# A transformer block in fp32: two token tiles per step in one projection, an earlier start in the other, and a residual handed to ScalarE and Pool

## The chip, the cores and the metric

The kernel runs on one core of a Trainium2 chip. A core has five engines that this document names: TensorE (PE; its weight loads are listed apart as PEld), VectorE (DVE), ScalarE (ACT), Pool (POOL) and the queue of DMA issues SP. Each engine works through its own instructions in order and waits on semaphores for the others. The metric is the time of one execution on the device in microseconds (us), as the median of several.

## The reference

The input is `h` of shape 8 x 1024 x 512, in fp32: eight sequences of 1024 tokens with 512 features. Every sequence goes through a block with a norm before and after each part:

```python
x = h
x = x + layernorm(attention(layernorm(x), Wqvk, Wo))
x = x + layernorm(ffn(layernorm(x), W1, b1, phases, w_real, w_imag, W2, b2))

# attention: 16 heads of 32 features, causal, softmax(q k / sqrt(512)) v, then Wo
# ffn:
hidden = x @ W1 + b1                                   # 512 -> 2048
imag   = w_imag * sin(phases + 0.1 * hidden)
phase  = cos(phases) * w_real + sin(phases) * w_imag   # per feature
act    = relu(hidden + 0.1 * phase * imag)
y      = act @ W2 + b2                                 # 2048 -> 512
```

`layernorm` subtracts the mean over the 512 features and divides by the root of the variance plus 1e-5; it has no weights of its own.

## The kernel before

The sequences are worked on one after the other. A token tile is 128 tokens (128 partitions) by 512 features, so a sequence has 8 tiles and a half of a sequence has 4. The running `x` of a sequence lies in SBUF in 8 tiles.

**Attention** (`attention`, L666) takes the 16 heads in 4 groups of 4 heads (`g` = 0 to 3). A group has two stages. `find_maxima` (L434) multiplies queries and keys once to get the row maxima: TensorE writes scores into PSUM banks (L473), VectorE reduces them with the mask (L503) or without (L491), ScalarE takes exponentials for one half (L523), and `split` brings the maxima into three bf16 parts, for one half on Pool (L451 to L460), which TensorE then transposes (L106). Four runs of this stage are filled up with steps of `work`, the projection of queries, keys and values for the next group (L374, L395). The second stage multiplies again with the maxima already subtracted, in units of key blocks: 3 units for the first half of the queries (`c` = 0), 7 for the second (`c` = 1), counted through as `at` = 0 to 9. For each unit `weigh` does the product (L577, L588), the exponential on ScalarE (L603) and on Pool the causal cut of the diagonal blocks (a select, L607). `weighted_values` (L626) follows one unit later. In the second half VectorE adds the weights of all units up (`add_weights`, L655); at the end of the group TensorE sums them over keys with a matmul of ones (L641), and `divide` takes Ln and Exp on ScalarE and multiplies on VectorE (L660 to L663). In a group that is not the last this happens inside the first run of the next group's maxima.

**The projection with Wo and the norms around it** (`finish_block`, L751) exist once for each half. For each of the 4 tiles: TensorE projects (L761), ScalarE copies the result out of PSUM (L770), VectorE takes mean and variance (`moments`, L218 and L219), Pool computes the reciprocal root (`rstd_of`, L225 and L226, a pair of instructions), VectorE normalises (L230) and adds to `x` (L281); then mean and variance of the new `x`, again the pair on Pool, the normalisation into `xn` (L230), four transposes on TensorE (L106), and ScalarE's copy into `x2T` (L248), the right side of the feed-forward.

**The feed-forward** (`feed_forward`, L785) takes 16 chunks of 128 hidden features for each half, 32 in all. `hidden` multiplies with W1 (L806) and lets ScalarE and VectorE form the activation (L814 to L825); `accumulate` multiplies with W2 into four PSUM banks (L833), two chunks later (`LAG`). `end(half)` adds the bias b2 on VectorE (L847), normalises and adds to `x` (L230, L281), stores `x` to DRAM through SP and loads the next sequence's tile there (L853, L113).

**What sets the order.** Side work is written as generators: `staged` runs the stages of successive tiles one step apart, later stages first within a step, and `advance` takes one step of such work at a chosen place. Instructions marked `in_order` keep their place in the program on their engine; the others may be moved by the scheduler of the framework, which orders each engine's queue before the run. TensorE's instructions are all in order. Three pieces of side work matter here:

- `finish_block` for half 0 runs during group 3, one step after each unit from `at` = 4 on. It has 8 steps for 4 tiles, so six run in the units, one after them, and one after the sums.
- `finish_block` for half 1 (`between`) runs in the feed-forward, one step per chunk, after the accumulation:

```python
if c >= LAG:
    accumulate(c - LAG)
...
elif c > 1:
    advance(between)
    advance(rest)
```

- `end(1)` of a sequence is left over (`rest`) for group 0 of the next sequence. Its four bias additions are issued at the end of the feed-forward, its steps from `at` = 3 on (`if g == 0: return rest, len(KEY_UNITS[0])`).

The buffers for `yp`, `xn`, `yb`, `inverse` and reloaded input come from a pool of 5 tiles, those of weights, scores and hidden chunks from a pool of 7.

## Time and profile before

| | |
|---|---|
| Time, median of 3 runs | 3938.61 us (3938.57 to 3939.71) |
| The profiled execution | 3939.17 us, span of its instructions 3937.4 us |
| Granted TensorE clock | 0.997 of full speed |
| Busy: PE, DVE, ACT, POOL | 97%, 71%, 38%, 14% of the span |
| Start of the feed-forward, sequences 1 to 5 | 1269.25, 1755.55, 2241.86, 2728.16, 3214.46 us: one sequence takes 486.3 us |
| Chain that ended last, by engine | PE 85%, DVE 9%, ACT 2%, issue 2%, POOL 2% |
| Largest groups on PE | L806 919.0 us, L833 691.3 us, L374 480.9 us |

Lines of the profile read as follows. In the list of waits: the engine, what it wrote and on which line, an arrow to the one that released it, the sum of the idle time, how often, and the longest, in us. In the timeline: the start in us from the first instruction, the duration from the first to the last of a run of equal instructions, the engine, the line, the operation, what it writes and reads, the shapes, the count, and in brackets the idle time of the engine just before with what ended it. In the list of groups: the busy time of all, the mean duration of one in ns, and the idle time before them. An fp32 matmul stands as two instructions, so the four products of a tile show as x8. A matmul's end is modelled, so its duration overlaps the next one's start; the distance from start to start tells the pace.

### The profile page before, as it was taken

Reading aid. Unit: us, or ns where it says so; the run is one execution under the profiler, and the core shown is the slowest. Engines: PE = TensorE matmul, PEld = TensorE weight load, DVE = VectorE, ACT = ScalarE, POOL = GpSimd, SP = SyncE. Lnnn points to the kernel's source line nnn. Section 1 sums busy time; section 2 is a strip of 40 time slices with the busy share of each in tenths; the row PEclk is TensorE's granted clock in tenths of the full one; section 3 lists DMA queues with packets and bytes.
Section 4 is the critical chain, followed back from the end, with each engine's and each line's share of the span. In section 5 each row is a group of like instructions: output and inputs, shape, how many; then the busy total and the mean of one; then the engine's idle time right before and its main releaser. Section 6 shows DMA issues by size and latency. Waiting matters only on the chain.

```text
span 3937.4 us, 51398 instructions
## 1 busy us (share of the span) xinstructions
PE 3810.8 (97%) x19457; PEld 1759.9 (45%) x19457; DVE 2792.0 (71%) x6161; ACT 1504.8 (38%) x2804; POOL 545.7 (14%) x1131
## 2 busy tenths in 40 slices
PE   8999999999999999999999999999999999999998
PEld 4444444444444444444444444444444444444343
DVE  4777767777777777777777677766777766777666
ACT  4552145521465214642146421454214642155321
POOL 1220011200112001120012100111001120021200
PEclk9999999999999999999999999999999999999999
DMA  4000000000000001000000000000001000000000
GB/s 153 25 20 22 22 17 25 15 22 22 28 17 12 22 22 33 12 12 22 22 33 12 12 22 22 33 12 12 22 22 33 12 12 0 22 23 12 1 0 22
DMA packets 43496, 86.43 MB, mean 22 GB/s; under 512 B 4144, under 2 KB 4208, under 8 KB 42736
## 3 DMA queue, kind: packets, MB, share of 16 engines
q1 hardware_dynamic: 39056, 71.61, 5.6%
q10 hardware_dynamic: 4192, 11.53, 0.8%
q8 instruction: 152, 2.49, 0.3%
q14 instruction: 96, 0.79, 0.1%
HBM read 66.36 MB, written 16.78 MB: 21 GB/s over the span
## 4 chain that ended last, share of the span: by engine, by line
PE 85%; DVE 9%; ACT 2%; issue 2%; POOL 2%; DMA 0%; POOLq 0%; SPq 0%; DVEq 0%
PE banks L833 22%; PE banks L806 22%; PE banks L374 11%; PE banks L473 7%; PE banks L395 6%; PE banks L761 4%; PE banks L588 4%; PE banks L626 4%; DVE w L655 3%; PE banks L577 2%; DVE mx L491 2%; PE banks L106 2%; ACT w L603 1%; PE banks L641 1%; DVE st L218 1%
## 5 line engine op out<-in xcount | busy, mean ns | idle before, releaser
L806 PE MATMUL banks<-x2T,w_sb 128*128 128x512 f32 x2048 | 919.0, 593 | 5.4 <-ACT x2T L248 5.4
L833 PE MATMUL banks<-w_sb,hid 128*128 128x512 f32 x1536 | 691.3, 593 | 8.9 <-DVE hid L825 8.9
L603 ACT ACTIVATE w<-banks 128x1024 f32<-128x1024 f32 (+1 forms) x640 | 566.1, 937 | 284.4 <-PE banks L588 274.7
L806 PEld LDWEIGHTS banks<-x2T,w_sb 128*128 128x128 f32 x2048 | 386.0, 190 | 478.0 <-issue 468.8
L655 DVE TENSOR_TENSOR w<-w 128x1024 f32<-128x1024 f32 (+2 forms) x448 | 444.2, 1030 | 199.3 <-PE banks L626 168.3
L503 DVE CUSTOM_DVE_ANT_0 es<-banks,mask 128x128 f32<-128x128 f32 (+3 forms) x1024 | 432.6, 485 | 121.6 <-PE banks L473 121.6
L821 ACT ACTIVATE u<-u 128x512 f32<-128x512 f32 x256 | 161.1, 629 | 853.6 <-DVE u L189 853.5
L374 PE MATMUL banks<-xnT,wqvk_sb 128*128 128x512 f32 x1024 | 480.9, 609 | 3.0 <-DVE mx L491 3.0
L833 PEld LDWEIGHTS banks<-w_sb,hid 128*128 128x128 f32 x1536 | 291.2, 190 | 379.1 <-issue 335.1
L491 DVE TENSOR_REDUCE mx<-banks 128x1 f32<-128x512 f32 (+1 forms) x384 | 309.7, 861 | 116.9 <-PE banks L473 116.9
L607 POOL TENSOR_SCALAR_AFFINE_SELECT w<-w 128x256 f32<-128x256 f32 x512 | 292.6, 593 | 671.8 <-ACT w L603 664.1
L814 ACT ACTIVATE hid<-banks,prm 128x512 f32<-128x512 f32 x256 | 175.6, 686 | 502.2 <-PE banks L806 502.2
L626 PE MATMUL banks<-w,v 128*32 128x512 f32 (+3 forms) x3072 | 329.0, 496 | 22.8 <-POOL w L607 22.1
L588 PE MATMUL banks<-qk 32*128 32x512 f32 (+3 forms) x3072 | 327.9, 491 | 0.0
L816 DVE TENSOR_SCALAR u<-hid,prm 128x512 f32<-128x512 f32 x256 | 123.7, 483 | 282.5 <-ACT hid L814 282.1
L473 PE MATMUL banks<-qk 32*128 32x512 f32 (+3 forms) x3072 | 314.0, 513 | 0.3 <-DVE mx L503 0.2
L824 DVE SCALAR_TENSOR_TENSOR hid<-u,coef,hid 128x512 f32<-128x512 f32 x256 | 192.0, 750 | 162.7 <-ACT u L821 162.7
L374 PEld LDWEIGHTS banks<-xnT,wqvk_sb 128*128 128x128 f32 x1024 | 182.8, 190 | 243.3 <-issue 182.9
L523 ACT ACTIVATE es<-es,mx 128x512 f32<-128x512 f32 (+3 forms) x512 | 279.6, 550 | 2.0 <-DVE mx L503 2.0
L395 PEld LDWEIGHTS banks<-wqvk_sb,xnT 128*128 128x128 f32 x2048 | 239.0, 192 | 57.9 <-issue 34.4
L395 PE MATMUL banks<-wqvk_sb,xnT 128*128 128x128 f32 x2048 | 259.5, 280 | 0.0
L761 PE MATMUL banks<-wo_sb,wvT 128*128 128x512 f32 x512 | 233.5, 599 | 0.0
(96 smaller groups left out, 3371.2 us busy)
## 6 DMA issues: line engine op xcount, KB each, us to landing
xin<-in_L_attn_h_dram SPq DMA_DIRECT2D x112, 256.0 KB, 2.7
x<-in_L_attn_h_dram SPq DMA_DIRECT2D x64, 256.0 KB, 2.6
out_dram<-x SPq DMA_DIRECT2D x64, 256.0 KB, 2.0
w_tail<-in_L_ffn_W_dram SPq DMA_DIRECT2D x8, 1024.0 KB, 5.3
w_sb<-in_L_ffn_W_dram ACTq DMA_DIRECT2D x1, 4096.0 KB, 15.5
wqvk_sb<-in_L_attn_Wqvk_dram ACTq DMA_DIRECT2D x3, 1024.0 KB, 9.5
w_sb<-in_L_ffn_W_dram ACTq DMA_DIRECT2D x1, 3072.0 KB, 25.6
wo_sb<-in_L_attn_Wo_dram ACTq DMA_DIRECT2D x1, 1024.0 KB, 5.9
```

The lines of the kernel that those rows point to most:

```text
L374: nc.tensor.matmul(pq, wqvk_sb[:, kc, c0 : c0 + P], xnT[b, half][:, kc, :], start=(kc == 0), stop=(kc == KC - 1),)
L395: nc.tensor.matmul(pv[:, t - t0, :], xnT[b, t // TPB][:, kc, (t % TPB) * P : (t % TPB + 1) * P], wqvk_sb[:, kc, c0 : c0 + P], start=(kc == 0),
L473: nc.tensor.matmul(scs[j // 2][:, j % 2, at : at + n], t[r, 0, i * P : (i + 1) * P], t[r, 1, k0 : k0 + n], start=True, stop=True,)
L491: nc.vector.tensor_reduce(out=mx[:, m], in_=sc[:, m, cols], op=ALU.min, axis=mybir.AxisListType.X,)
L503: nc.vector.tensor_tensor_reduce(out=es[:, m, cols], in0=sc[:, m, cols], in1=mask[:, HALF - n :], scale=1.0, scalar=FMAX, op0=ALU.add, op1 ...
L588: nc.tensor.matmul(sts[j // 2][:, j % 2, cols], t[r, 1, kb * P : (kb + 1) * P], t[r, 0, q0 : q0 + n], start=False, stop=True,)
L603: in_order(nc.scalar.activation(w[:, :, :width], st[:, :, :width], AF.Exp, scale=-1.0))
L626: nc.tensor.matmul(acc[r, HALF - n :], v[b, g][:, kb, r], weights[j // 2][:, j % 2, cols], start=first and k == 0, stop=last and k == len( ...
L655: in_order(nc.vector.tensor_add(t[:, :, q], t[:, :, q], w[:, :, cols]))
L761: nc.tensor.matmul(y, wvT[:, kc, t * P : (t + 1) * P], wo_sb[:, kc, :], start=(kc == 0), stop=(kc == KC - 1),)
L806: nc.tensor.matmul(ph, w1_sb[:, kc, fc * P : (fc + 1) * P], x2T[half][:, kc, :], start=(kc == 0), stop=(kc == KC - 1),)
L833: nc.tensor.matmul(ys[half, t], hids[c // 2][:, c % 2, t * P : (t + 1) * P], w2_sb[:, fc, :] if fc < NW2 else w2_tail[:, fc - NW2, :], sta ...
```

## The change

Four things are done.

1. `finish_block` gets a parameter `by`, the number of tiles per step. Half 0 is done with two tiles per step: two projections in a row, one pair of Pool instructions for both tiles' roots, and so on. The measuring of the new `x` is a stage of its own. With 2 steps' worth of tiles and 5 stages there are 6 steps. Half 1 keeps one tile per step.
2. In the feed-forward the steps of half 1 begin with chunk 0 instead of chunk 2, and for the chunks 0 to 2 they stand before the accumulation instead of behind it.
3. `end(1)` of all sequences but the last (`spare`) copies the result out of PSUM on ScalarE, adds the bias on Pool and adds the normalised result to `x` on Pool. The copies and Pool's additions are in order.
4. In group 0 the steps of that residual are taken from the first run of the maxima on (four steps there, the other two from `at` = 3 on).

The normalisation stays on VectorE in all of them, and the sums, products and stores are the same as before. The diff, cut to its core:

```diff
@@ rstd_of
-            rs = small.tile([P, n], F32, tag=f"rs{n}", name="rs")
+            rs = small.tile([P, n], F32, tag=f"rs{n}", name="rs", bufs=4 // n)
@@ find_maxima, at the end of each of its four runs
             advance(work, fill)
+            advance(more)
@@ attention
         for g in range(NG):
-            mT, later = find_maxima(b, g, work, sums)
+            more, first = after(g)
+            mT, later = find_maxima(b, g, work, sums, more if g == 0 else iter(()))
             mTs = [mT]
-            more, first = after(g)
@@ finish_block
-        def project(t):
-            y = psum([P, D])
-...
-        measure, add = residual_stages(x, lambda t: ys[t])
-        return staged(
-            TPB,
-            lambda t: (project(t), measure(t)),
-            add,
-            *norm_stages(x, False, lambda t: x2T[half][:, :, t * P : (t + 1) * P], nc.scalar.copy),
-        )
+        def tiles(n):
+            return range(n * by, (n + 1) * by)
+
+        def measure(n, source):
+            mvs[n] = small.tile([P, by, 2], F32, tag=f"mv{by}", name="mv", bufs=6 // by)
+            for t in tiles(n):
+                moments(source(t), mvs[n][:, t - n * by, :])
+            rss[n] = rstd_of(mvs[n], by)
+
+        def project(n):
+            for t in tiles(n):
+                y = psum([P, D])
+                for kc in range(KC):
+                    in_order(nc.tensor.matmul(y, ...))
+                ys[t] = tmp.tile([P, D], F32, tag="tmp", name="yp")
+                nc.scalar.copy(ys[t], y)
+                drained(y)
+            measure(n, lambda t: ys[t])
+
+        def add(n):
+            for t in tiles(n):
+                in_order(normalise(n, t, ys[t], ys[t]))
+                in_order(nc.vector.tensor_add(x(t), x(t), ys[t]))
+
+        def scale(n):
+            for t in tiles(n):
+                xns[t] = tmp.tile([P, D], F32, tag="tmp", name="xn")
+                normalise(n, t, xns[t], x(t))
+
+        def transpose(n):
+            for t in tiles(n):
+                transpose_rows(xns[t], x2T[half][:, :, t * P : (t + 1) * P], nc.scalar.copy)
+
+        return staged(TPB // by, project, add, lambda n: measure(n, x), scale, transpose)
@@ feed_forward, end(half)
+            spare = half and b + 1 < B
...
-                nc.vector.tensor_add(yb, ys[half, t], b2_sb)
+                if spare:
+                    in_order(nc.scalar.copy(yb, ys[half, t]))
+                    in_order(nc.gpsimd.tensor_tensor(yb, yb, b2_sb, ALU.add))
+                else:
+                    nc.vector.tensor_add(yb, ys[half, t], b2_sb)
...
+            def add(t):
+                in_order(normalised(ybs[t], ybs[t], mvs[t], rss[t]))
+                if spare:
+                    in_order(nc.gpsimd.tensor_tensor(x(t), x(t), ybs[t], ALU.add))
+                else:
+                    in_order(nc.vector.tensor_add(x(t), x(t), ybs[t]))
@@ feed_forward, the loop over chunks c
             if c < 2 * NFC:
                 hidden(c)
+            if c <= LAG:
+                advance(between)
             if c >= LAG:
                 accumulate(c - LAG)
             if c - LAG == NFC - 1:
                 rest = end(0)
-            elif c > 1:
+            elif c > LAG:
                 advance(between)
                 advance(rest)
@@ the two calls
-                return finish_block(b, 0, wvT[0], x2T), len(KEY_UNITS[0]) + 1
+                return finish_block(b, 0, wvT[0], x2T, 2), len(KEY_UNITS[0]) + 1
...
-        rest = feed_forward(b, x2T, finish_block(b, 1, wvT[1], x2T))
+        rest = feed_forward(b, x2T, finish_block(b, 1, wvT[1], x2T, 1))
```

More of the change, by code (lines that the diff above doesn't have):

```diff
@@ L249, in transpose_rows, with norm_stages @@
         drained(pt)
-    def norm_stages(source, own, dst, evacuate):
+    def norm_stages(source, dst, evacuate):
         mvs, rss, xns = {}, {}, {}
@@ L261, in scale @@
         def scale(t):
-            xns[t] = source(t) if own else tmp.tile([P, D], F32, tag="tmp", name="xn")
+            xns[t] = tmp.tile([P, D], F32, tag="tmp", name="xn")
             normalised(xns[t], source(t), mvs[t], rss[t])
@@ L268, in norm_stages @@
         return measure, scale, transpose
-    def residual_stages(target, y):
-        mvs, rss = {}, {}
-        def measure(t):
-            mvs[t] = one_mv()
-            moments(y(t), mvs[t][:, 0, :])
-            rss[t] = rstd_of(mvs[t], 1)
-        def add(t):
-            in_order(normalised(y(t), y(t), mvs[t], rss[t]))
-            in_order(nc.vector.tensor_add(target(t), target(t), y(t)))
-        return measure, add
     def advance(work, steps=1):
@@ L317, in norm1_first @@
         dst = new_xnT(0)
-        return staged(NT, *norm_stages(lambda t: xt[0, t], False, dst, nc.scalar.copy))
+        return staged(NT, *norm_stages(lambda t: xt[0, t], dst, nc.scalar.copy))
     moments_ahead = {}
@@ L432, with find_maxima @@
     )
-    def find_maxima(b, g, work, sums):
+    def find_maxima(b, g, work, sums, more):
         t = qk[b, g]
@@ L749, in attention, with finish_block @@
             finish(more)
-    def finish_block(b, half, wvT, x2T):
+    def finish_block(b, half, wvT, x2T, by):
         x2T[half] = tp.tile([P, KC, HALF], F32, tag="t", name=f"x2T_{b}_{half}")
-        ys = {}
-        def project(t):
-            y = psum([P, D])
-            for kc in range(KC):
-                in_order(
-                    nc.tensor.matmul(
-                        y,
-                        wvT[:, kc, t * P : (t + 1) * P],
-                        wo_sb[:, kc, :],
-                        start=(kc == 0),
-                        stop=(kc == KC - 1),
-                    )
-                )
-            ys[t] = tmp.tile([P, D], F32, tag="tmp", name="yp")
-            nc.scalar.copy(ys[t], y)
-            drained(y)
+        ys, xns, mvs, rss = {}, {}, {}, {}
+        def tiles(n):
+            return range(n * by, (n + 1) * by)
@@ L773, in x @@
         def x(t):
             return xt[b, half * TPB + t]
-        measure, add = residual_stages(x, lambda t: ys[t])
-        return staged(
-            TPB,
-            lambda t: (project(t), measure(t)),
-            add,
-            *norm_stages(x, False, lambda t: x2T[half][:, :, t * P : (t + 1) * P], nc.scalar.copy),
-        )
+        def measure(n, source):
[3 more added lines that the diff above has]
+            rss[n] = rstd_of(mvs[n], by)
@@ new lines, in normalise @@
+        def normalise(n, t, dst, src):
+            m = t - n * by
+            return normalised(dst, src, mvs[n][:, m : m + 1, :], rss[n][:, m : m + 1])
+        def project(n):
+            for t in tiles(n):
+                y = psum([P, D])
+                for kc in range(KC):
+                    in_order(
+                        nc.tensor.matmul(
+                            y,
+                            wvT[:, kc, t * P : (t + 1) * P],
+                            wo_sb[:, kc, :],
+                            start=(kc == 0),
+                            stop=(kc == KC - 1),
+                        )
+                    )
+                ys[t] = tmp.tile([P, D], F32, tag="tmp", name="yp")
+                nc.scalar.copy(ys[t], y)
+                drained(y)
+            measure(n, lambda t: ys[t])
@@ new lines, in add @@
+        def add(n):
[4 more added lines that the diff above has]
+            for t in tiles(n):
+                xns[t] = tmp.tile([P, D], F32, tag="tmp", name="xn")
+                normalise(n, t, xns[t], x(t))
+        def transpose(n):
+            for t in tiles(n):
+                transpose_rows(xns[t], x2T[half][:, :, t * P : (t + 1) * P], nc.scalar.copy)
@@ L846, in end, with x, measure @@
                 yb = tmp.tile([P, D], F32, tag="tmp", name="yb")
-                nc.vector.tensor_add(yb, ys[half, t], b2_sb)
+                if spare:
[3 more added lines that the diff above has]
+                    nc.vector.tensor_add(yb, ys[half, t], b2_sb)
                 drained(ys[half, t])
                 ybs.append(yb)
+            def x(t):
+                return xt[b, half * TPB + t]
+            mvs, rss = {}, {}
+            def measure(t):
+                mvs[t] = one_mv()
+                moments(ybs[t], mvs[t][:, 0, :])
+                rss[t] = rstd_of(mvs[t], 1)
+            def add(t):
[4 more added lines that the diff above has]
+                    in_order(nc.vector.tensor_add(x(t), x(t), ybs[t]))
             def store(t):
@@ L855, in store @@
                     load_x(b + 1, i)
-            return staged(
-                TPB,
-                *residual_stages(lambda t: xt[b, half * TPB + t], lambda t: ybs[t]),
-                store,
-            )
+            return staged(TPB, measure, add, store)
         rest = iter(())
```

## The prediction

> **What bounds the kernel now.** I read the page first, then TensorE's waits, then the order of time around each wait, engine by engine. TensorE is busy for 97% of the span, so a change pays only where it waits. Three waits belong to the places the change touches.

> ```profile
> PE 3810.8 (97%) x19457; PEld 1759.9 (45%) x19457; DVE 2792.0 (71%) x6161; ACT 1504.8 (38%) x2804; POOL 545.7 (14%) x1131
> ```
> ```profile
> PE banks L626 <- POOL w L607: 22.1, 34, 1.0
> PE banks L641 <- DVE w L655: 12.0, 7, 1.7
> ...
> PE banks L833 <- DVE hid L825: 8.9, 8, 1.1
> ```

> Seven waits at L641: once per sequence but the first, in head group 0, where the residual of the previous sequence runs. Eight at L833: the first accumulation of each feed-forward. The 34 at L626 are about four per sequence, at the end of attention (group 3), where no projection work fills the gaps. A wait's figure is not its whole price, because a matmul that is held up inside its group counts as busy. Group 1 does what group 0 does without the residual, so the two are compared from the same instruction to the same instruction:

> ```profile
> 1060.80 1.06 PE L626 MATMUL banks<-w,v 128*32 128x512 f32 x8
> ...
> 1080.58 1.56 PE L641 MATMUL banks<-w,ones 128*32 128x512 f32 x8 [1.72 <-DVE w L655]
> 1082.08 1.16 PE L395 MATMUL banks<-wqvk_sb,xnT 128*128 128x128 f32 x8
> ```
> ```profile
> 1118.62 1.06 PE L626 MATMUL banks<-w,v 128*32 128x512 f32 x8
> ...
> 1136.90 2.05 PE L395 MATMUL banks<-wqvk_sb,xnT 128*128 128x128 f32 x16
> ```

> Group 0 takes 21.28 us, group 1 18.28: the residual costs 3.00, not the 1.72 of the wait. Next, TensorE and VectorE at the end of attention of sequence 0:

> ```profile
> 748.36 3.70 PE L761 MATMUL banks<-wo_sb,wvT 128*128 128x512 f32 x8
> 751.99 0.39 PE L577 MATMUL banks<-mT,minus 32*128 32x512 bf16 x4
> ...
> 773.98 0.84 PE L626 MATMUL banks<-w,v 128*32 128x384 f32 x4 [0.99 <-POOL w L607]
> ...
> 782.94 10.57 PE L806 MATMUL banks<-x2T,w_sb 128*128 128x512 f32 x24 [0.67 <-ACT x2T L248]
> 794.62 1.55 PE L833 MATMUL banks<-w_sb,hid 128*128 128x512 f32 x3 [1.12 <-DVE hid L825]
> ```
> ```profile
> 748.53 2.36 DVE L655 TENSOR_TENSOR w<-w 128x1024 f32<-128x1024 f32 x2 [5.12 <-PE banks L626]
> 752.72 0.69 DVE L218 BATCH_NORM_STATS2 st<-yp 128x6 f32<-128x512 f32 x1 [1.82 <-ACT yp L770]
> ...
> 780.41 0.53 DVE L230 TENSOR_SCALAR xn<-x,mv,rs 128x512 f32<-128x512 f32 x1
> ```

> Each projection of a tile (eight instructions, 3.43 us within a stream, 3.63 with the switch of tile shape) stands alone between two units of attention. The feed-forward starts at 782.94; three chunks need 3 x 3.43 = 10.30, so the first accumulation could start at 793.24 and starts at 794.62: 1.38 lost per sequence.

> **Part 1: first accumulation (second half projected from chunk 0).** Three projections now stand between the first chunks: six blocks of 3.43 = 20.6 us pass before the first accumulation, while its hidden chunk is ready 794.57 - 782.94 = 11.6 after the start (last L825 before the wait). No TensorE work is added; it is moved from behind the accumulations. The first projection needs the divided head group 3 only in its fourth quarter, 3.43 + 2.57 = 6.0 after the start; Ln, Exp and multiply (0.60, 0.63, 0.69 and their hand-overs) take 2.5. VectorE has about 4.8 per chunk and 3.5 per residual tile in 6.86 per block pair; it may fall behind by a microsecond per step, but the second accumulation is due only after 27 us and two chunks lie in hand, so I cost that at nothing. ScalarE's four copies move with them, at 38% busy. -1.38 x 8 = **-11.0**; between -8.9 (the wait alone) and -11.9 (the 0.11 that the first block runs long as well).

> **Part 2: residual end in group 0.** What goes: the eight DVE operations between the additions L655, and with them 3.00 x 7 = **-21.0** (12.0 if only the wait goes). What comes instead, in program order:
> - ScalarE copies four PSUM tiles (0.59 each, from 1017.28). The table load that stood at 1014.28 comes behind them, at about 1020.5, and ends at 1021.8. Cover: ScalarE's next work is at 1024.56, after 9.00 idle. Without that cover 1.3 x 7.
> - Pool adds the bias, four times. No row has such an addition. Pool's select takes 0.41 for 256 elements and 0.295 for 128: 0.64 for 512 with one input, the lower end. [...] VectorE stands still here, so I take 1.2.
> - VectorE's statistics of the four tiles stand in its queue ahead of the first maxima (L503). It waits there for Pool: the first maximum starts at 1017.95 + 4d + 0.65, and the last bank of the first run is free 2.74 later (1021.72 to 1024.46), at 1021.3 + 4d. TensorE needs it for the second piece of the second run, 1026.24 + 0.97 = 1027.2. So d up to 1.47 is hidden; at 1.2 it is free at 1026.1. Cost nothing; the margin is 1.1.
> - Four normalisations (0.54) between maxima: the gaps there are 0.70 and 0.39, then 2.46 and 5.12. At most 0.15.
> - On Pool, the second x addition (from 1038.6, 1.2) and a rstd pair (0.87) stand before the split of the maxima, which began at 1040.35 and now begins near 1040.8; the transposes behind it come 0 to 0.45 later. I take 0.3 x 7 = **+2**.
> - SP's stores and loads go out earlier and nobody waits for them.

> ```profile
> L607 POOL TENSOR_SCALAR_AFFINE_SELECT w<-w 128x256 f32<-128x256 f32 x512 | 292.6, 593 | 671.8 <-ACT w L603 664.1
> ...
> L460 POOL TENSOR_TENSOR mx<-mx,parts_q 128x16 f32<-128x16 f32 x64 | 14.7, 230 | 5.1
> ```
> ```profile
> 1024.56 0.60 ACT L385 ACTIVATE qk<-banks 128x512 f32<-128x512 f32 x1 [9.00 <-PE banks L374]
> ```

> [...]

> **Part 3: two tiles at a time in group 3.** The pairs save 2 x 0.20 of switching on TensorE, but TensorE is not last there. VectorE's work stays the same: from 748.53 to 780.94 are 32.41 us, of which 1.82 + 0.80 + 0.56 + 0.87 + 0.86 + 0.87 = 5.78 idle, so 26.63 work. In the changed order it idles:
> - 1.83 until the first copy (752.72);
> - 2.5 from 753.62 until the second tile's copy, since its statistics come next in the queue (projection one block later: 756.15);
> - 0.8 until the next unit's exponentials (757.86);
> - 2.0 from 763.4 to 765.4: the fourth tile's statistics stand ahead of the first tile's second ones, and its projection ends near 764.7;
> - 0.3 and 0.9 for two rstd on Pool (two elements each, 0.9 to 1.4).

> Together 8.3. End: 748.53 + 26.6 + 8.3 + 0.3 for Pool's last selects = 783.7. Now the sums L641 follow these last additions directly: in group 0 that took from 1081.04 to 1082.08, 1.04. So the feed-forward starts at 784.75 instead of 782.94: +1.8 x 8 = **+14.4**. The transposes no longer end last; the additions do. Who waits: the sums, and behind them everything on TensorE. From below: if all six waits of this stage went (0.99 + 0.51 + 0.67 + 0.45 + 0.67 + 0.67), -4.0 per sequence. From above: rstd 0.65 + 1.40 from 776.2, six selects at 1.02, a last addition 0.8 and 1.04: 786.2, +3.3. The count of VectorE is nearest, because every term is a row of this stage.

> [...] The rows differ: beside selects L655 went from 1.16 to 1.23, the selects from 0.41 to 1.02. [...]

> **Sum.** -11.0 - 21.0 + 2.0 + 14.4 = -15.6. The profiled execution took 3939.17 (span 3937.4 and 1.8 around it), 0.56 over the median of 3938.61. 3939.17 - 15.6 - 0.56 gives **3923.0**, 0.4% faster. A measurement of this kernel can tell about 0.2%, 7.9 us.

> **Rivals.**
> - *Attention ends no later* (the 2.0 and 2.5 of idle are filled): part 3 at nothing, 3909. For it: the chain of the last tile starts 5 us earlier than before. Against: VectorE's queue is in order.
> - *Attention ends 3.3 to 3.7 later*: Pool's selects and rstd are the bound. 3923 + 8 x 1.7 = 3936.6, no difference that counts. For it: selects of 1.02 in groups 0 and 1. Against: in group 1 six selects took 4.69 in all.
> - *Slower*: Pool's bias addition is long, and VectorE stands before the first maxima. Each sequence but the first pays 4d - 5.9: at d = 3.0 6.1 x 7 = 43, 3966. It decides from d = 2.3 on, where 3.3 x 7 = 23.5 eats the gain and 0.2%. Against: nothing of VectorE runs beside it.
> - *The move does nothing for the first accumulation*, since another wait takes its place (the divided group): 3934.

> **How the numbers follow.** Forecast 0.60; earlier end 0.12; late end 0.14; the long addition 0.08; no gain at the accumulation 0.06. The forecast alone spans 3914 to 3931. The range of 3909 to 3938 leaves out the long addition and half of the earliest case. Faster: 0.60 + 0.12 + a little of the late end = 0.75; within 0.2% 0.16; slower 0.09.

> **What would show it.** Right: the wait of L833 on L825 gone; no wait of the sums on VectorE in group 0, and its stretch near 18.3; the sums of group 3 waiting for the additions, and the feed-forward 1 to 3 us later after the first projection (34.6 before). Pool's 128x512 addition shows at 1.1 to 1.4. Wrong: the first maxima of a sequence beginning after 1025 in this time base, or first chunks with VectorE behind.

## The result, and the profile after

| | before | after |
|---|---|---|
| Time, median | 3938.61 us (five runs, 3938.53 to 3940.46) | 3954.46 us (five runs, 3953.17 to 3956.03) |
| Ratio | | 1.0039, 95% interval 1.0024 to 1.0053 |
| The profiled execution, its span, granted clock | 3939.17, 3937.4, 0.997 | 3953.17, 3951.4, 0.989 |
| First projection of group 3 to the feed-forward, sequence 1 (TensorE) | 748.36 to 782.94: 34.58 | 748.59 to 788.26: 39.67 |
| The same, mean of the eight sequences | 34.59 (34.58 in six of them) | 40.12 |

The change makes the kernel 0.4% slower, where 0.4% faster was forecast: 3923.0 within 3909 to 3938. Sequences are counted from 0 here, so the feed-forward at 782.94 is that of sequence 1; the prediction calls it sequence 0, and the five starts listed ahead of it belong to the sequences 2 to 6. Busy time by engine, on the page of the profile after:

```profile
PE 3818.5 (97%) x19457; PEld 1765.7 (45%) x19457; DVE 2762.2 (70%) x6105; ACT 1525.1 (39%) x2832; POOL 599.3 (15%) x1123
```

TensorE issues the same 19457 matmuls and is busy 7.7 us longer with them: some took longer (those of 128x384 for the weighted values 542 ns on average, 498 before). Its waits after:

```profile
PE banks L106 <- DVE xn L230: 34.8, 9, 17.3
PE banks L612 <- POOL w L593: 26.7, 10, 3.2
...
PE banks L764 <- ACT yp L773: 10.8, 16, 0.7
```

Two of the three waits that the forecast aimed at are gone: no row of the sums (now L627) for VectorE's weights, and none of the accumulation (now L842) for the hidden chunk. The third, for Pool's weights (now L612), was 22.1 us in 34 pieces of at most 1.0; it is now 10 pieces of up to 3.2. New are nine waits of the transposes for `xn` (one of 17.3 at the very start of the kernel, the other eight 2.2 each) and sixteen waits of a projection for ScalarE's copy, two per sequence.

In group 0 (timeline of TensorE, columns as explained for the profile before) the stretch is now that of group 1:

```profile
1065.01 1.06 PE L612 MATMUL banks<-w,v 128*32 128x512 f32 x8
...
1083.30 2.05 PE L380 MATMUL banks<-wqvk_sb,xnT 128*128 128x128 f32 x16
```

18.29 us in place of 21.28. The end of attention, TensorE:

```profile
748.59 3.70 PE L764 MATMUL banks<-wo_sb,wvT 128*128 128x512 f32 x8
752.97 3.70 PE L764 MATMUL banks<-wo_sb,wvT 128*128 128x512 f32 x8 [0.68 <-ACT yp L773]
...
776.69 0.63 PE L106 MATMUL banks<-ident,xn 128*128 128x128 f32 x4 [2.18 <-DVE xn L230]
...
781.20 3.01 PE L612 MATMUL banks<-w,v 128*32 128x384 f32 x16 [3.23 <-POOL w L593]
...
788.26 3.70 PE L815 MATMUL banks<-x2T,w_sb 128*128 128x512 f32 x8
...
808.97 3.60 PE L842 MATMUL banks<-w_sb,hid 128*128 128x512 f32 x8
```

The two projections of a pair do not run on: the second starts 4.38 after the first, not 3.43. Later TensorE waits 2.18 and 3.23, and the 16 matmuls of L612 that follow take 2.94 from start to start, although they are of the size that took 1.06 for 12 before; at full clock, in a run below (TensorE kept busy), the same 16 take 2.30, so Pool's selects hold them up as well. The first accumulation (L842) has no wait any more. VectorE and Pool in the same stretch:

```profile
757.33 0.69 DVE L218 BATCH_NORM_STATS2 st<-yp 128x6 f32<-128x512 f32 x1 [3.47 <-ACT yp L773]
...
767.51 0.70 DVE L218 BATCH_NORM_STATS2 st<-yp 128x6 f32<-128x512 f32 x1 [2.93 <-ACT yp L773]
...
780.80 1.17 DVE L230 TENSOR_SCALAR xn<-x,mv,rs 128x512 f32<-128x512 f32 x2 [0.60 <-POOL rs L226]
781.89 4.51 DVE L641 TENSOR_TENSOR w<-w 128x768 f32<-128x768 f32 x6
```
```profile
778.04 1.10 POOL L225 TENSOR_SCALAR rs<-mv 128x2 f32<-128x2 f32 x1 [5.23 <-DVE mv L219]
779.23 1.54 POOL L226 TENSOR_TENSOR rs<-rs,mhalf 128x2 f32<-128x2 f32 x1
780.74 4.18 POOL L593 TENSOR_SCALAR_AFFINE_SELECT w<-w 128x256 f32<-128x256 f32 x6
```

VectorE idles 3.47 and 2.93 where 2.5 and 2.0 were forecast. Its last additions L641 end at 786.40; 783.4 was forecast before Pool's last selects, 783.7 with them. And the granted clock, the share of its full speed that the profile records for TensorE, in five windows of 3.41 us (columns: window and its length, busy time and count of PE, PEld, DVE, ACT, POOL, the granted clock, share of DMA, GB/s):

```profile
771.99:775.41 3.42, 2.52 (x32) 1.15 (x24) 3.42 (x5) 2.80 (x4) 0.42 (x2) 1.00 0.00 0
775.41:778.82 3.41, 1.28 (x16) 0.74 (x16) 3.41 (x8) 1.26 (x3) 0.78 (x1) 1.00 0.00 0
778.82:782.23 3.41, 1.03 (x4) 0.19 (x4) 2.81 (x5) 0.60 (x1) 3.33 (x6) 0.50 0.86 285
782.23:785.65 3.42, 3.02 (x18) 1.41 (x16) 3.21 (x5) 0.36 (x1) 2.69 (x3) 0.50 0.06 23
785.65:789.06 3.41, 3.03 (x22) 1.23 (x23) 0.75 (x2) 1.42 (x4) 0.00 (x0) 1.00 0.02 5
```

TensorE's clock is halved from 778.82 to 785.65. This happens at the end of attention of every sequence, for 6.83 us in five of them and 10.24 in three; in the trace of before it does not happen there at all. Where it lasts 10.24 the stretch takes 40.9 to 41.1, otherwise 39.4 to 39.7. But the trace of before has such a fall elsewhere, besides those near the kernel's start and end: 13.65 us from 3629.86 on, among the first scores of head group 3 in the last sequence, where no projection for a next group fills the gaps (windows of before, columns as above):

```profile
3626.44:3629.86 3.42, 3.41 (x13) 1.34 (x12) 3.42 (x9) 3.18 (x12) 0.00 (x0) 1.00 0.00 0
3629.86:3633.27 3.41, 3.41 (x19) 2.56 (x20) 3.41 (x8) 1.84 (x7) 0.00 (x0) 0.50 0.00 0
```

TensorE counts as busy throughout, but with 13 instructions in 3.42 us, where 16 score matmuls of 32x512 take 1.93 in group 0 (1026.24 to 1028.17): they are held up inside their group. This fall was there to be seen before the forecast, and all runs have it, for 6.8 to 13.7 us (10.24 in the changed kernel, from 3642.60 on).

### The profile page after: what moved, and what is told of

Its sections match the earlier page's. It is cut to its first block, busy times and chain, and to the rows that moved or that the text cites. A ratio compares the mean times of both kernels' runs of the same rounds, so it can differ in the third digit from the quotient of the medians.

```text
span 3951.4 us, 51420 instructions
## 1 busy us (share of the span) xinstructions
PE 3818.5 (97%) x19457; PEld 1765.7 (45%) x19457; DVE 2762.2 (70%) x6105; ACT 1525.1 (39%) x2832; POOL 599.3 (15%) x1123
## 4 chain that ended last, share of the span: by engine, by line
PE 90%; DVE 4%; ACT 2%; issue 2%; POOL 1%; DMA 0%; POOLq 0%; SPq 0%; DVEq 0%
PE banks L815 22%; PE banks L842 22%; PE banks L359 12%; PE banks L458 7%; PE banks L380 6%; PE banks L764 6%; PE banks L612 5%; PE banks L574 5%; PE banks L563 2%; PE banks L106 2%; DVE mx L476 2%; ACT w L589 1%; PE banks L627 1%; POOL rs L226 1%; DVE st L218 1%
## 5 line engine op out<-in xcount | busy, mean ns | idle before, releaser
L842 PE MATMUL banks<-w_sb,hid 128*128 128x512 f32 x1536 | 692.6, 593 | 0.1
L641 DVE TENSOR_TENSOR w<-w 128x1024 f32<-128x1024 f32 (+2 forms) x448 | 447.2, 1036 | 203.8 <-PE banks L612 165.3
L842 PEld LDWEIGHTS banks<-w_sb,hid 128*128 128x128 f32 x1536 | 291.2, 190 | 370.2 <-issue 329.3
L593 POOL TENSOR_SCALAR_AFFINE_SELECT w<-w 128x256 f32<-128x256 f32 x512 | 281.4, 568 | 655.0 <-ACT w L589 649.2
L612 PE MATMUL banks<-w,v 128*32 128x512 f32 (+3 forms) x3072 | 331.3, 508 | 26.7 <-POOL w L593 26.7
L825 DVE TENSOR_SCALAR u<-hid,prm 128x512 f32<-128x512 f32 x256 | 123.9, 484 | 292.2 <-ACT hid L823 292.1
L833 DVE SCALAR_TENSOR_TENSOR hid<-u,coef,hid 128x512 f32<-128x512 f32 x256 | 192.2, 751 | 161.8 <-ACT u L830 161.1
L225 POOL TENSOR_SCALAR rs<-mv 128x1 f32<-128x1 f32 (+1 forms) x168 | 66.3, 394 | 1302.5 <-DVE mv L219 1297.5
```

The source lines that it names most:

```text
L593: select = nc.gpsimd.affine_select(out=square, in_=square, compare_op=ALU.is_ge, fill=0.0, base=0, pattern=[[0, 2], [1, P]], channel_multi ...
L612: nc.tensor.matmul(acc[r, HALF - n :], v[b, g][:, kb, r], weights[j // 2][:, j % 2, cols], start=first and k == 0, stop=last and k == len( ...
L641: in_order(nc.vector.tensor_add(t[:, :, q], t[:, :, q], w[:, :, cols]))
L842: nc.tensor.matmul(ys[half, t], hids[c // 2][:, c % 2, t * P : (t + 1) * P], w2_sb[:, fc, :] if fc < NW2 else w2_tail[:, fc - NW2, :], sta ...
```

## The experiments

The forecast has three parts, and for the third there are three suspected causes. Diffs are against the changed kernel unless another is named. All ratios are to the kernel before, measured on the same chip: it took 3939.2 to 3939.6 there, and 3938.6 beside the changed kernel, so a difference to the changed kernel carries about 1 us. "Stretch" is the time from the first projection of group 3 to the feed-forward, as in the table above.

### One tile at a time, the other parts kept

```diff
-                return finish_block(b, 0, wvT[0], x2T, 2), len(KEY_UNITS[0]) + 1
+                return finish_block(b, 0, wvT[0], x2T, 1), len(KEY_UNITS[0]) + 1
```

> The changed kernel with the first half projected and normed one tile at a time again; the second half between first chunks and the residual by ScalarE and Pool stay. Theory (the pairs cost all that was lost): group 0 keeps its 18.29 us (-3.0 x 7 = -21), the first accumulation keeps its place (-1.1 x 8 = -9), the first projection to the feed-forward is back at 34.6 us: 3908.6, between 3905 and 3913. Rival (the pairs cost the 1.8 per sequence that was forecast, the rest of the loss came from the other two parts): 3954.5 - 8 x 1.8 = 3940, between 3935 and 3945.

Measured: 3911.09 us beside 3939.61, ratio 0.9927 (0.9912 to 0.9942). The stretch is 34.58 to 34.60 in every sequence and the clock keeps at 1.00 there. All of the loss came with the pairs; without them the change gains 0.7%.

### The pairs alone

```diff
-            mT, later = find_maxima(b, g, work, sums, more if g == 0 else iter(()))
+            mT, later = find_maxima(b, g, work, sums, iter(()))
...
-            spare = half and b + 1 < B
+            spare = False
...
-            if c <= LAG:
-                advance(between)
...
-            elif c > LAG:
+            elif c > 1:
```

> The kernel before with the pairs of the first half only: VectorE alone does the residual between groups, the second half's projections stand behind the accumulations as before. Theory: the first projection to the feed-forward takes 39.4 to 41.1 us in place of 34.6, 5.1 to 6.5 per sequence, 3938.6 + 45 = 3984, between 3977 and 3990, and the granted clock falls to half once per sequence near the end of attention. Rival (forecast's 1.8 per sequence): 3953, between 3948 and 3958. If the clock falls only where the other parts have changed the work around, the time lies between them, near 3965.

Measured: 3979.68 us, ratio 1.0102 (1.0087 to 1.0117). The stretch is 39.4 to 39.7 in all eight sequences, mean 39.58, and the clock is halved for 6.83 in each. (39.58 - 34.58) x 8 = 40.0, and 3979.68 - 3939.61 = 40.1: the stretch is the whole loss. It needs neither of the other parts.

### The earlier first half of the feed-forward alone, the residual alone

Both do one tile at a time. The first has, besides, `spare` = False and no residual steps in the runs of the maxima; the second has the old loop over chunks instead:

```diff
-            if c <= LAG:
-                advance(between)
...
-            elif c > LAG:
+            elif c > 1:
```

> The kernel before with the second half's projections and residual steps placed from the first chunk of the feed-forward on, and nothing else. Theory (the three parts add up): the first accumulation no longer waits, 1.1 us per sequence as in the trace of the changed kernel, 8 x 1.1 = 9 below the kernel before: 3930.6 beside 3939.6 (3928 to 3933). Rival (the gain needs the other parts, or was given back by VectorE's later work): 3937 to 3940.

> The kernel before with the residual end of a sequence by ScalarE and Pool, and nothing else. Theory (the parts add up): group 0 falls from 21.28 to 18.29 us in seven sequences, 21 below the kernel before: 3918.6 beside 3939.6 (3916 to 3921). Rival (Pool's additions and the later first maxima take part of it): only the wait of 1.72 goes, 12 below, 3927.

Measured: 3931.28 us (ratio 0.9979, 0.9970 to 0.9989) and 3918.68 us (0.9947, 0.9932 to 0.9962) beside 3939.42: -8.1 and -20.7, both within what was expected. Together -28.9; with one tile at a time both gave -28.5. With the stretch of the changed kernel, (40.12 - 34.58) x 8 = +44.3, the three make +15.4 over 3939.4: 3954.8, and it measured 3954.46. The parts add up, and the sum closes.

### Two banks for the two projections of a pair

`psum` hands out banks in the order of the program; the second projection gets the bank that ScalarE is just copying the first one out of.

```diff
+            banks_y = {t: psum([P, D]) for t in tiles(n)}
             for t in tiles(n):
-                y = psum([P, D])
+                y = banks_y[t]
```

> The changed kernel with both PSUM tiles of a pair's projections taken before the first is written, so that they lie in two banks. Theory: the wait of 0.68 us of the second projection on ScalarE's copy goes (0.95 with the switch, twice per sequence), the second tile's statistics on VectorE come 0.95 earlier, and with them the last normalisations: -0.95 to -1.9 per sequence, 3939 to 3947, 3943 likeliest, with the clock's fall still there. If the stage no longer falls to half the clock, another 3 per sequence: 3919. Rival (the end is set by Pool's last selects behind the root, which the banks do not move): 3951 to 3955.

Measured: 3937.21 us, ratio 0.9993 (0.9983 to 1.0002): 17.3 below the changed kernel and 1.8 below the range that was expected. Now the pair runs on in TensorE's timeline, and VectorE's idle times before the second statistics are those of the forecast:

```profile
749.29 7.13 PE L765 MATMUL banks<-wo_sb,wvT 128*128 128x512 f32 x16
...
786.72 3.70 PE L816 MATMUL banks<-x2T,w_sb 128*128 128x512 f32 x8
```
```profile
757.08 0.69 DVE L218 BATCH_NORM_STATS2 st<-yp 128x6 f32<-128x512 f32 x1 [2.52 <-ACT yp L774]
...
766.32 0.69 DVE L218 BATCH_NORM_STATS2 st<-yp 128x6 f32<-128x512 f32 x1 [1.98 <-ACT yp L774]
```

The stretch is 37.2 to 37.5 where the clock is halved for 6.83, and 39.2 where it is halved for longer; the mean is 38.06, 2.06 less than in the changed kernel. The fall of the clock stays.

### TensorE kept busy

```diff
+    def keep_busy(n):
+        pad = psum([P, HALF])
+        for _ in range(n):
+            in_order(nc.tensor.matmul(pad, ident, wo_sb[:, 0, :], start=True, stop=True))
+        drained(pad)
...
+                    if g == NG - 1 and at == 9:
+                        keep_busy(3)
                     flush()
...
             for t in tiles(n):
+                if by == 2 and t == 1:
+                    keep_busy(2)
                 transpose_rows(xns[t], ...)
```

> The changed kernel with five more fp32 matmuls of 128x512 (0.43 us each) per sequence at the end of attention: two ahead of the second tile's transposes of the first pair (where TensorE waited 2.18 us), three ahead of the values of the last unit but two (where it waited 3.23). They write a PSUM bank that nobody reads; the result is computed as before. Theory (TensorE's idle time makes the granted clock fall to half for 6.8 to 10.2 us, which costs 3 to 4.5 us per sequence): the clock stays at 1.00 in this stage, and the stage falls from 39.4-41.1 us to 36-37.5: 3954.5 - 8 x 3.5 = 3926, between 3919 and 3935. Rival (the waits alone set the end, the clock is low where TensorE has little to do anyway): 3954 to 3960.

Measured: 3943.81 us, ratio 1.0010 (1.0001 to 1.0019): 10.7 below the changed kernel, with more matmuls than it. No fall of the clock in any of the eight stretches, and all take 38.84 or 38.85. So the fall is made by TensorE's idle time and costs 40.12 - 38.85 = 1.27 per sequence, 10.2 in all. That is little more than a third of what I expected: the rest of the stretch is not the clock. What sets the end shows in the timelines of VectorE and TensorE (L656 is the first two additional matmuls; each stands as two instructions, so one takes about twice the 0.43 of the expectation):

```profile
782.59 4.52 DVE L641 TENSOR_TENSOR w<-w 128x768 f32<-128x768 f32 x6
```
```profile
776.24 1.98 PE L656 MATMUL banks<-wo_sb,ident 128*128 128x512 f32 x4 [1.03 <-ACT x2T L248]
...
787.07 1.15 PE L627 MATMUL banks<-w,ones 128*32 128x512 f32 x8
788.14 3.70 PE L826 MATMUL banks<-x2T,w_sb 128*128 128x512 f32 x8
```

VectorE's last addition ends at 787.11, 37.82 after the first projection (749.29); in the changed kernel it was 786.40 - 748.59 = 37.81. The matmuls did nothing for VectorE. The feed-forward follows 1.03 behind that end here and 1.86 behind it in the changed kernel: at half the clock TensorE has a tail of its own.

### Only the later three additional matmuls

Against the kernel of the section above:

```diff
-                if by == 2 and t == 1:
-                    keep_busy(2)
```

> The changed kernel with only the three later additional matmuls (ahead of the values of the last unit but two, where TensorE waited 3.23 us); they write a PSUM bank that nobody reads, the result is computed as before. Theory (the idle time ahead of the fall, the 2.18 at the second tile's transposes, sets it off): the fall of the clock at the same place stays in every sequence, and at most its length drops to 6.83 us: 3948 to 3954. Rival (the longer wait of 3.23 sets it off): no fall, 3944.

Measured: 3943.83 us, ratio 1.0010 (1.0001 to 1.0019), the stretch 38.86 in all sequences. The clock is halved for 3.41 in five of the eight stretches and not at all in three, and neither costs anything. The time is the rival's, but my theory was wrong and the rival only half right: without the longer wait the fall comes only in some of the sequences and, where it comes, is over before it matters. Whether it came went with how the wait lies in the windows of 3.41 us on the trace's own grid of clock changes (view of windows, columns as above), here sequence 0 and then sequence 1:

```profile
287.94:291.35 3.41, 1.37 (x17) 0.83 (x17) 3.41 (x8) 1.47 (x4) 0.03 (x1) 1.00 0.00 0
291.35:294.76 3.41, 3.41 (x4) 1.38 (x5) 2.81 (x4) 1.13 (x2) 3.33 (x4) 0.50 0.63 196
772.63:776.04 3.41, 1.65 (x12) 0.56 (x8) 3.41 (x5) 2.43 (x3) 0.00 (x0) 1.00 0.00 0
776.04:779.45 3.41, 2.98 (x20) 1.61 (x21) 3.41 (x7) 1.71 (x3) 1.56 (x2) 1.00 0.12 17
```

The same wait of about 2.2 us lies nearly whole in one window in the first case (1.37 busy, half the clock next); in the second a border cuts it (1.65 and 2.98 busy, full clock). The other six go the same way: 1.23 or 1.24 busy and half the clock in four, 1.81 and 1.96 busy and full clock in two.

### Both causes away: two banks and kept busy

The two edits together, with the bank of the additional matmuls taken earlier and four of them in the first place, so that they wait for no copy:

```diff
+            pad = psum([P, HALF]) if by == 2 and n == 0 else None
             for t in tiles(n):
+                if pad is not None and t == 1:
+                    keep_busy(4, pad)
```

> The changed kernel with both causes taken away at once: the two projections of a pair in two PSUM banks, and seven more fp32 matmuls of 128x512 per sequence (four ahead of the second tile's transposes of the first pair, three ahead of the values of the last unit but two) into a bank that nobody reads; the result is computed as before. Theory (banks, clock and VectorE's own order add up): no fall of the clock, VectorE's chain ends 35.95 us after the first projection as with the two banks alone, and the sums 1.04 later: 37.0 us for the stage in every sequence, 3911.1 + 8 x (37.0 - 34.6) = 3930 (3927 to 3934). Rival (the clock costs nothing once the banks no longer delay VectorE, since VectorE sets the end): the stage stays at 37.3 to 37.5, 3934 to 3938. What is left over the kernel with one tile at a time, 2.4 per sequence, would be the idle time of VectorE's queue that the forecast counted.

Measured: 3927.54 us, ratio 0.9971 (0.9960 to 0.9982), the stretch 36.96 to 36.98 in every sequence, the clock at 1.00. Theory right, to 0.03 us per sequence. This is what the forecast had in mind: VectorE's order alone, 36.97 - 34.58 = 2.4 per sequence. With the banks taken away first, they are worth 40.12 - 38.06 = 2.06 and the clock 38.06 - 36.97 = 1.09; with the clock first, 1.27 and 1.88. The two overlap by 0.2.

```profile
776.46 1.17 DVE L230 TENSOR_SCALAR xn<-x,mv,rs 128x512 f32<-128x512 f32 x2 [0.60 <-POOL rs L226]
777.55 4.51 DVE L641 TENSOR_TENSOR w<-w 128x768 f32<-128x768 f32 x6
```
```profile
782.02 1.15 PE L627 MATMUL banks<-w,ones 128*32 128x512 f32 x8
783.10 3.70 PE L827 MATMUL banks<-x2T,w_sb 128*128 128x512 f32 x8
```

The last additions end at 782.06 and the feed-forward starts 1.04 later.

### Projected one at a time, normed two at a time

What is left of the loss: is it the two projections in a row, or the norming by twos?

```diff
+            for s in range(2 * TPB):
+                n, odd = divmod(s, 2)
...
+                if s < TPB:
+                    project(s)
+                if odd and n < TPB // by:
+                    measure(n, lambda t: ys[t])
+                yield True
```

> The changed kernel with the first half projected one tile per unit of attention, as in the kernel before, while the normings still take two tiles at a time (one root for two tiles on Pool; addition, second statistics, scaling and transposes for two). Theory (two projections in a row keep VectorE idle and are what is left of the loss; the norming by twos costs little): the first projection to the feed-forward takes 34.6 to 36.0 us, 3911 to 3923, 3917 likeliest, no fall of the clock. Rival (the norming by twos is the loss: one long turn of VectorE and the roots ahead of the last selects): 37 us or more, 3930 and up.

Measured: 3928.66 us, ratio 0.9972 (0.9961 to 0.9983), between both. In the three stretches without a fall of the clock it takes 36.32, in the five with a fall of 3.41 us 37.1 to 37.4. So norming by twos costs 36.32 - 34.58 = 1.7 in this order of the steps, and I was wrong to think it cheap. The last two tiles come at once, behind everything that Pool and VectorE do for the last units (TensorE):

```profile
778.60 1.05 PE L627 MATMUL banks<-w,ones 128*32 128x512 f32 x4 [1.60 <-DVE w L641]
779.90 1.05 PE L627 MATMUL banks<-w,ones 128*32 128x512 f32 x4 [0.25 <-DVE w L641]
780.89 1.09 PE L106 MATMUL banks<-ident,xn 128*128 128x128 f32 x8
783.22 3.70 PE L836 MATMUL banks<-x2T,w_sb 128*128 128x512 f32 x8 [1.24 <-ACT x2T L248]
```

With one tile at a time the third tile's transposes and copy lie before the sums, and one copy alone ends last. Here two do. The order of the last steps differs from that of the pairs, so the 0.65 that is left to 36.97 is only roughly the price of two projections in a row. The opposite, two projections in a row and one tile normed at a time, was not run.

### A long addition on Pool

The rival "slower" of the forecast, measured on the kernel with one tile at a time:

```diff
-                    in_order(nc.scalar.copy(yb, ys[half, t]))
+                    in_order(nc.scalar.mul(yb, ys[half, t], 0.5))
+                    in_order(nc.gpsimd.tensor_tensor(yb, yb, yb, ALU.add))
                     in_order(nc.gpsimd.tensor_tensor(yb, yb, b2_sb, ALU.add))
```

> The kernel with one tile at a time, in which Pool's part of the bias addition is made twice as long: ScalarE writes half of each PSUM tile, Pool adds the tile to itself (exact) and then the bias, 2 x 1.27 us per tile in place of 1.27; the result is computed as before. It measures the rival of the long addition in the forecast. Theory (VectorE's statistics stand in its queue ahead of the first maxima, hidden up to 1.47 per tile and 4 x d - 5.9 beyond): at d = 2.53 4.2 us per sequence, 7 x 4.2 = 29 above one tile at a time: 3940 (3936 to 3946), with TensorE waiting for VectorE's maxima at the start of each sequence. Rival (other work covers it, and Pool is free there): 3911 to 3914.

Measured: 3945.68 us, 34.6 above one tile at a time. Adding a tile to itself took less than expected, 1.04, so d is 2.34 from start to start and the forecast's 4d - 5.9 gives 3.5 per sequence. The wait is where it was expected (Pool, then TensorE):

```profile
1026.09 1.26 POOL L861 TENSOR_TENSOR yb<-yb,b_sb 128x512 f32<-128x512 f32 x1
```
```profile
1028.81 3.18 PE L458 MATMUL banks<-qk 32*128 32x512 f32 x12 [1.44 <-DVE mx L488]
```

From the feed-forward to the next first projection it takes 3.56 and 3.54 longer than with the single addition in the two sequences in which the clock does not fall there (451.28 against 447.72 and 439.27 against 435.73), and 5.2 in the five in which it is halved for 3.41 us. So the rival's formula holds where the clock stays, the true addition (1.27) lies within the 1.47 that are hidden, and the clock adds half again.

### The sums' bank

With one tile at a time, the sums of group 3 wait 0.68 for a copy out of their bank. The bank is taken earlier:

```diff
+                            early = psum([P, HALF]) if g == NG - 1 else None
                             def whole():
-                                whole_sum = psum([P, HALF])
+                                whole_sum = early if early is not None else psum([P, HALF])
```

> The kernel with one tile at a time, in which the sums of the weights in the last head group take their PSUM bank ahead of the third tile's transposes, not behind them. Theory (the same kind of wait as in the pairs: 0.68 us of the sums for ScalarE's copy out of the bank that they are given, once per sequence, on TensorE's path): the stage falls from 34.59 by 0.4 to 0.7 us, 3 to 5.5 in all: 3906 to 3908. Rival (VectorE's last scaling sets the last transposes, and the wait only moves there): 3911.

Measured: 3909.90 us, ratio 0.9926 (0.9914 to 0.9939), not to be told from 3911.09; the stretch 34.51. The rival's time came: the wait only moves. The sums start without a wait and then take 1.50 from start to start, held up inside, where they took 0.99. What they wait for there is VectorE's last addition, which ends at 777.15, rather than the last scaling that the rival named:

```profile
776.68 1.56 PE L627 MATMUL banks<-w,ones 128*32 128x512 f32 x8
778.18 0.66 PE L106 MATMUL banks<-ident,xn 128*128 128x128 f32 x4
779.51 3.70 PE L817 MATMUL banks<-x2T,w_sb 128*128 128x512 f32 x8 [0.68 <-ACT x2T L248]
```

## Why the prediction was wrong, and where it was right

It failed at **part 3**: +14.4 was forecast, +44.3 came (5.54 per sequence, not 1.8). The steps, per sequence:

| | stretch | what it adds |
|---|---|---|
| before | 34.58 | |
| forecast | 36.4 | +1.8 |
| pairs with two banks, kept busy | 36.97 | +0.6: VectorE's work, mis-sized |
| pairs in one bank, kept busy | 38.85 | +1.88: the second projection's wait for its bank |
| changed kernel | 40.12 | +1.27: the fall of the clock |

- **"The second tile's statistics, projection one block later", 2.5 and 2.0.** The step that failed first. I let the second projection follow the first at 3.43 and did not ask which bank it gets. It waits 0.68 for the copy of the first (0.95 later in start), the idle times are 3.47 and 2.93, and as VectorE's queue is in order, both 0.95 come out at the end: 1.9, and 1.88 was measured.
- **The clock** was in no term. I took the granted clock of before, 1.00 in this stage, for given, although the change makes TensorE wait there in larger pieces. Thirty-four waits of 1.0 or less did not halve it; waits of 2.18 and 3.23 did. That it can fall inside this kernel the trace of before had shown, at 3629.86.
- **The count of VectorE** was right in its idle times: without the two omissions they are 1.82, 2.52, 0.80, 1.98 and 0.37 + 0.60 + 0.60, 8.7 together, against 1.83, 2.5, 0.8, 2.0 and 0.3 + 0.9, 8.3, and 0.3 for Pool's last selects, which shows in no wait. The 1.04 from the last addition to the feed-forward is exact. The stretch was short by 0.6, of which 0.45 is work: counted as in the forecast, as the time that is not idle, it is 35.77 - 8.69 = 27.1 with both causes away, not 26.6. What grew are the additions of the weights: the last six take 4.51 in one piece (from 777.55 above), where before they stood in two (VectorE):

```profile
775.87 2.53 DVE L655 TENSOR_TENSOR w<-w 128x768 f32<-128x768 f32 x3
...
778.87 1.61 DVE L655 TENSOR_TENSOR w<-w 128x256 f32<-128x256 f32 x3
```

- **"Beside selects L655 went from 1.16 to 1.23"** is misread. In the trace of before the addition of 128x1024 takes 1.21 to 1.23 everywhere but in group 0, beside the residual, where three in each sequence but the first take 1.42 or 1.43; the selects beside them take up to 1.50. So an addition took up to 0.2 longer there beside Pool's selects, and the forecast had it at nothing.
- **"From above +3.3"** was no bound. It varied only what VectorE and Pool do; the two terms from outside that list make 3.1 per sequence.
- **"The pairs save 2 x 0.20 on TensorE"**: wrong in sign, for the same reason as the first: the second projection starts 4.38 after the first, where 3.43 was meant and 3.63 is what a projection standing alone takes.

**Part 1**, -11.0: measured -8.1 alone. The wait went as forecast, and the first accumulation starts 20.71 after the feed-forward (six blocks, 20.6). Mis-sized is 1.38, the gain per sequence: 1.1 was measured on the trace of the changed kernel (226.4 to 225.3 from the feed-forward to the last accumulations) and 1.0 in the run of this part alone. Of the 1.38, 0.11 could not go: the first hidden block takes 3.54 from start to start and not 3.43, before and after alike. The 0.11 by which the first accumulation ran long did go in the changed kernel. But the accumulation at 924.02, at the change to the second half, takes 3.71 in place of 3.43: 1.38 - 0.11 + 0.11 - 0.28 = 1.10. What holds that one up inside, the trace does not say.

**Part 2**, -21.0 + 2.0: measured -20.7 alone, so the gain is right and the +2 for Pool's split was nothing (23.10 from the first scores to the transposes of the maxima, 23.09 before). The forecast's 1.2 for Pool's addition of 128x512 was an estimate that no run had shown; the runs showed 1.27:

```profile
L879 POOL TENSOR_TENSOR x<-x,yb 128x512 f32<-128x512 f32 x28 | 35.5, 1267 | 118.0 <-DVE yb L230 118.0
L860 POOL TENSOR_TENSOR yb<-yb,b_sb 128x512 f32<-128x512 f32 x28 | 34.6, 1267 | 642.4 <-ACT yb L859 642.4
```

**The rivals.** "Attention ends 3.3 to 3.7 later" had the right place and the wrong mechanism: Pool's roots and selects do stand late (1.10 and 1.54 beside VectorE's additions, selects from 780.74), but the two causes above decide. The price of the long addition was well set where the clock stays (3.5 forecast, 3.55 measured; 5.2 where it falls), but it did not occur. I had put the chance of slower, 9%, almost wholly on it, and gave none to the stage that I had just shown to be full of waits.

The version with one tile at a time, 3911 us, is faster than both kernels: it has the gains of parts 1 and 2 without the pairs.

## What to carry to other kernels

When work is batched two at a time, look up for each buffer which one the second item gets: with one bank for two projections in a row the second waited 0.68 here, and the stretch fell by 1.88 when it had its own. Where an engine works in order and ends last, ask where the time that it idles early comes out: VectorE idled 0.95 longer twice, and 1.88 of it came out at the end. And gathering small waits of TensorE into larger ones cost 1.27 per sequence beyond the waits here, so read the granted clock in the stage where they will lie and keep a place for it in the sum.
